# An LSTM on one core: other layouts and queues for the loads of Wx, Wh, x and h0 before the first step

## The chip, the core and the metric

The kernel runs on one core of a Trainium2 chip. A core has a matrix engine (PE, TensorE), a vector engine (DVE, VectorE), a scalar engine (ACT, ScalarE), GpSimd (POOL) and a queue engine that issues transfers (SP, SyncE). They run their own instruction streams and meet through semaphores. Transfers (DMAs) are issued by SP, ACT or POOL, and 16 DMA engines carry them between HBM and the on-chip memory SBUF, which has 128 partitions. Matmul results land in PSUM.

The metric is the device time in microseconds (us) of one execution. The profile's clock starts at the first instruction, and its "span" ends with the last one.

## The reference, cut to what matters

There are 16 sequences of 512 steps with 512 features; the hidden width is also 512. All data is float32.

```python
xW = einsum('ntd,dg->ntg', x, Wx) + b          # Wx: 512 x 2048
def step(carry, xw_t):
    prev_h, prev_c = carry
    a = xw_t + prev_h @ Wh                      # Wh: 512 x 2048
    i, f, o = sigmoid(a[:, :512]), sigmoid(a[:, 512:1024]), sigmoid(a[:, 1024:1536])
    g = tanh(a[:, 1536:])
    next_c = f * prev_c + i * g
    next_h = o * tanh(next_c)
    return (next_h, next_c), next_h
out = x + scan(step, (h0, 0), xW over t)        # h0 is cond_1024, 16 x 512
```

The 512 steps depend on each other through `h`. Before the first one, Wx (4 MB), Wh (4 MB), the first slice of x (256 KB), h0 (32 KB) and the bias must have come from HBM.

## The kernel before

**The loop.** `lstm_residual` (line 38 on) keeps the four gates of the 16 sequences in PSUM banks, with the width split into two halves, a and b, that work a little apart. Each of the 512 steps multiplies the previous h, as parts in float16, with `wq`, Wh split into three float16 parts (`products`, the matmuls of line 188), and in between projects x of a later pair of steps with Wx in float32 (`project`, line 165). DVE and ACT do the gates. `turn_x` (line 161) transposes the x of one pair of steps on DVE in 32 x 32 blocks, once in two steps. The order on every engine is that of the program; the framework adds the waits.

**The stretch before the loop.** Wh is loaded to `wh_sb` (line 134, in `load_w`) in eight copies of 512 KB, four from SP's queue and four from ACT's, each for a block of 32 partitions: the rows of two of the four 32-row chunks `c` that each block has. Chunks 0 and 1 come with the first four copies, chunks 2 and 3 with the second. Behind them, SP issues the eight copies of the first x slice (`load_xs(0)`, line 147), four of h0 (line 347), eight of Wx (line 134 again, 32 partitions each) and eight of the second x slice. POOL issues the bias as one row (`brow`, line 348) and as a tile (`bias`, line 352), and the other eight copies of Wx. ACT then loads its function table (line 371).

While a queue's instruction waits, everything behind it in that queue waits too. The framework gives each transfer one of a fixed set of completion semaphores in turn, and the next user of a semaphore waits until its last user has landed.

**The split of Wh.** `bound(c)` finds the largest magnitude in each row of chunk c (lines 397 to 399; ACT does chunk 1, DVE the others), `scales(h)` makes scale factors from the bounds of two chunks (lines 410 to 422), and `split(n, k)` with k = 0 to 4 makes the three float16 parts of half-chunk n (n = 0 to 7): k = 0, 2, 4 on ACT (lines 432, 439, 444), k = 1, 3 on DVE (lines 435, 442). A loop over n interleaves them. In it are also the three `turn_x` of the first x slice and the transpose of h0 to `hT0` (line 470), at n = 3 before the change; the first two projections (64 matmuls) and 16 matmuls of zeros (line 374) for PE, written at n = 4; and `seed(0, h)` (line 175, ACT), which puts the projection into the gates, at n = 6. The first step then starts on PE with `first_products` (line 201), which needs seeds and `hT0`.

Of the kernel before, what the change touches and what calls it, by code (L numbers as in the profile page):

```python
# [7 lines left out]
FP = mybir.dt.float32  # L8
HP = mybir.dt.float16
I32 = mybir.dt.int32  # L10
AF = mybir.ActivationFunctionType
ALU = mybir.AluOpType
PSUM = bass.MemoryType.PSUM

P = 128
Q = 32
# [15 lines left out]
def lstm_residual(ctx: ExitStack, tc: tile.TileContext, x, h0, wx, wh, b, out):  # L32
# [26 lines left out]
    nc = tc.nc  # L59
    N, T, D = x.shape  # L60
    H = h0.shape[1]
    NJ = H // P
    NK = D // P
    G = 4
    U = P // 2
    GU = G * U
    GH = G * H // 2
# [7 lines left out]
    const = ctx.enter_context(tc.tile_pool(name="const", bufs=1))  # L75
    tmp = ctx.enter_context(tc.tile_pool(name="tmp", bufs=3))
# [19 lines left out]
    wx_sb = const.tile([P, NK, G * H], FP, tag="wx", name="wx_sb")  # L96
    wh_sb = const.tile([P, NK, G * H], FP, tag="wh", name="wh_sb")
    wq = [const.tile([P, NK, G * H], HP, tag=f"wq{i}", name=f"wq{i}") for i in range(3)]

    wx_j = wx_sb.rearrange("p c (g j w) -> p c j g w", g=G, j=NJ)  # L100
    wh_j = wh_sb.rearrange("p c (e g j h u) -> p c e h j g u", e=2, g=2, j=NJ, h=2)
    wq_j = [w.rearrange("p c (g j h u) -> p c h j g u", g=G, j=NJ, h=2) for w in wq]
    bias = const.tile([P, G * P], FP, tag="bias", name="bias")
    mask = const.tile([P, S2], FP, tag="mask", name="mask")
    zero = const.tile([1, G * P], HP, tag="zero", name="zero")
    amax = const.tile([P, NK], FP, tag="amax", name="amax")
    top = const.tile([P, 2], FP, tag="top", name="top")
    bits = const.tile([P, 2, 2], FP, tag="bits", name="bits")
    sc = const.tile([P, 2, 4], FP, tag="sc", name="sc")
# [4 lines left out]
    parts = [  # L114
        [const.tile([P, 2, 5 * N], HP, tag=f"parts{h}{i}", name=f"parts{h}{i}") for i in range(2)]
        for h in range(2)
    ]
# [3 lines left out]
    ]  # L121
    xb = [psum.tile([P, G * P], FP, tag=f"xb{i}", name=f"xb{i}") for i in range(NXB)]

    def load_w(dst, w, c0, dmas, parts=1):


        n = G * H // parts
        for j in range(2):
            for q, dma in enumerate(dmas):
                r = w[(2 * q + j) * P + c0 * Q :][: 2 * Q].rearrange("(c u) f -> u c f", u=Q)  # L130
                p = slice((2 * q + j) * Q, (2 * q + j + 1) * Q)
                for e in range(parts):
                    a = parts - 1 - e
                    dma.dma_start(  # L134
                        out=dst[p, c0 : c0 + 2, a * n : (a + 1) * n],
                        in_=r[:, :, e * n : (e + 1) * n],
                    )

    xs = {}

    def load_xs(s, dma=nc.sync):

        xs[s] = xsp.tile([P, XP, P], FP, tag="xs", name=f"xs_{s}")
        for j in range(NJ):
            for r in range(S2):
                p0 = j * Q + r * N
                dma.dma_start(
                    out=xs[s][p0 : p0 + N],
                    in_=x[:, s * XB + r : (s + 1) * XB : S2, j * P : (j + 1) * P],
                )  # L150


    xT = {}
# [4 lines left out]
    def turn_x(q):  # L158
        s, i = divmod(q, XP)
        xT[q] = xtp.tile([P, NK, Q], FP, tag="xT", name=f"xT_{q}")  # L160
        nc.vector.transpose(xT[q].rearrange("p c m -> p (c m)"), xs[s][:, i])

    def project(q, c):
        for j in range(NJ):
            nc.tensor.matmul(  # L165
                xb[q % NXB][j * Q : (j + 1) * Q],
                lhsT=xT[q][:, c],
                rhs=wx_j[:, c, j],
                start=False,
                stop=(c == NK - 1),  # L170
                skip_group_check=True,
            )

    def seed(t, h):
        nc.scalar.mul(  # L175
            gates[h][t % 2][:, :GU].rearrange("p (g u) -> p g u", g=G),
            xb[t // 2 % NXB].rearrange("p (g h u) -> p h g u", g=G, h=2)[:, h],
            mask[:, t % 2 : t % 2 + 1],
        )
# [157 lines left out]
    warm = const.tile([1, 1], FP, tag="warm", name="warm")  # L337
    brow = const.tile([1, G * H], FP, tag="brow", name="brow")
    ones = const.tile([1, Q], FP, tag="ones", name="ones")
    for c in (0, 2):  # L340
        load_w(wh_sb, wh, c, (nc.sync, nc.scalar))
    load_xs(0)
    nc.vector.memset(zero, 0.0)
    nc.vector.memset(h_in, 0.0)
    nc.vector.memset(ones, 1.0)
    for j in range(NJ):
        nc.sync.dma_start(out=h_in[j * Q : j * Q + N], in_=h0[:, j * P : (j + 1) * P])
    nc.gpsimd.dma_start(out=brow, in_=b.rearrange("(o f) -> o f", o=1))
    b_j = b.rearrange("(o e g j w) -> j e o g w", o=1, e=2, g=2, j=NJ)
    for j in range(NJ):  # L350
        for e in range(2):
            nc.gpsimd.dma_start(
                out=bias[j * Q : (j + 1) * Q, (1 - e) * GU : (2 - e) * GU].rearrange(
                    "p (g w) -> p g w", g=2
                ),
                in_=b_j[j, e].broadcast_to([Q, 2, P]),
            )
    for c in (0, 2):
        load_w(wx_sb, wx, c, (nc.sync, nc.gpsimd), 2)
    load_xs(1)  # L360

    for h in range(2):
# [10 lines left out]
    def zeros(bank, start):  # L373
        nc.tensor.matmul(  # L374
            bank, lhsT=zero[:, :P], rhs=zero, start=start, stop=start, skip_group_check=True
        )
# [14 lines left out]
                    skip_group_check=True,  # L391
                )

    def bound(c):
        if c == 1:
            junk = tmp.tile([P, G * H], HP, tag="junk", name="junk", bufs=1)
            nc.scalar.activation(junk, wh_sb[:, c], AF.Abs, accum_out=amax[:, c : c + 1])
        else:
            nc.vector.tensor_reduce(
                amax[:, c : c + 1],  # L400
                wh_sb[:, c],
                mybir.AxisListType.X,
                ALU.max,
                apply_absolute_value=True,
            )

    def scales(h):


        nc.vector.tensor_tensor(  # L410
            top[:, h : h + 1], amax[:, 2 * h : 2 * h + 1], amax[:, 2 * h + 1 : 2 * h + 2], ALU.max
        )
        t = top[:, h : h + 1].bitcast(I32)
        e, inv = bits[:, h, 0:1], bits[:, h, 1:2]
        nc.vector.tensor_scalar(
            inv.bitcast(I32), t, EXP, EXP, ALU.bitwise_and, ALU.bitwise_xor
        )
        nc.vector.tensor_scalar(e.bitcast(I32), t, EXP, None, ALU.bitwise_and)
        nc.vector.tensor_scalar(RS2[h], inv, 2.0**12, 0.5, ALU.mult, ALU.min)
        nc.vector.tensor_scalar(RS[h], inv, 2.0**13, 1.0, ALU.mult, ALU.min)  # L420
        nc.vector.tensor_scalar(S[h], e, 2.0**-14, 1.0, ALU.mult, ALU.max)
        nc.vector.tensor_scalar(RSL[h], RS[h], 1.0 / LO, None, ALU.mult)
# [3 lines left out]
    def split(n, k):  # L426

        c, e = divmod(n, 2)
        w = wh_sb[:, c, e * GH : (e + 1) * GH]
        f = [q[:, c, (1 - e) * GH : (2 - e) * GH] for q in wq]  # L430
        if k == 0:
            nc.scalar.mul(f[0], w, RS2[c // 2])
        elif k == 1:
            r1[n] = tmp.tile([P, GH], FP, tag="r1", name=f"r1_{n}")
            nc.vector.scalar_tensor_tensor(
                r1[n], w, RS[c // 2], f[0], ALU.mult, ALU.subtract
            )
        elif k == 2:
            nc.scalar.copy(f[1], r1[n])
        elif k == 3:  # L440
            r2[n] = tmp.tile([P, GH], FP, tag="r2", name=f"r2_{n}")
            nc.vector.tensor_tensor(r2[n], r1[n], f[1], ALU.subtract)
        else:
            nc.scalar.mul(f[2], r2[n], LO)

    NH = 2 * NK
    bound(0)
    bound(1)
    scales(0)
    split(0, 0)  # L450
    split(0, 1)
    split(1, 0)
    for n in range(NH):
        if n == 0:
            bound(2)
        if n == 2:
            bound(3)
            scales(1)
        if n + 1 < NH:
            split(n + 1, 1)  # L460
        split(n, 2)
        split(n, 3)
        if n:
            split(n - 1, 4)
        if n + 2 < NH:
            split(n + 2, 0)
        if n == 3:
            for q in range(3):
                turn_x(q)
            nc.vector.transpose(hT0.rearrange("p c m -> p (c m)"), h_in)  # L470
        if n == 4:
            for c in range(NK):
                for q in range(2):
                    project(q, c)

            for _ in range(16):
                zeros(xb[3], False)
        if n == 6:
            for h in range(2):
                seed(0, h)  # L480
# [4 lines left out]
    for t in range(T):  # L485
        s, ti = divmod(t, XB)
        q, half = divmod(t + 4, 2)
# [12 lines left out]
        for op in STEP.split():  # L500
            name, h = op.split("_")
# [4 lines left out]
        if t % 2:  # L506
            for h in range(2):
                unscale(t // 2, h)
            if q + 1 < NP:
                turn_x(q + 1)  # L510
        else:
            if q + 1 < NP:
                put_bias(q + 1)
            if t:
                residual(t // 2 - 1)
# [33 lines left out]
```

## Time and profile before

| | |
|---|---|
| median of 3 runs | 2294.34 us (2294.26 to 2299.03) |
| the profiled execution | 2294.09 us |
| its span | 2291.7 us |
| PE busy | 2249.4 us (98%) |
| DVE busy | 1952.7 us (85%) |
| ACT busy | 1838.1 us (80%) |
| first matmul of step 0 (line 201) starts at | 50.80 us |

The profiled execution is 2.4 us longer than its span; this lies outside of what the engines show. Times in the text are counted from the span's start. A line of the profile such as "12.74 1.91 ACT L397 ... x1" says that ACT began an instruction of line 397 at 12.74 us and that it took 1.91 us. "[4.07 <-DMA wh_sb...]" says that the engine had been idle for 4.07 us before it and that the landing of that transfer ended the idle time. "SPq" and "ACTq" are the instruction queues that issue transfers.

### The profile page before, as it was taken

How to read it: one execution, taken by the hardware profiler on the slowest of the kernel's cores; microseconds unless marked ns; L12 is line 12 of the kernel's file. 1: busy time of each engine (PE TensorE's matmuls, PEld its weight loads, DVE VectorE, ACT ScalarE, POOL GpSimd, SP SyncE). 2: the span in 40 equal slices, each digit the busy share in tenths (PEclk: the TensorE clock that was granted, in tenths of full speed). 3: DMA queues.
4: the chain of work that ended last, by engine and by line, in shares of the span. 5: the costliest groups of instructions: out<-in, count | busy, mean ns of one | idle time of the engine just before them, and what ended most of it. 6: DMA issues, size and time to landing. Idle time of an engine off the chain costs nothing.

```text
span 2291.7 us, 137735 instructions
## 1 busy us (share of the span) xinstructions
PE 2249.4 (98%) x57445; PEld 1572.7 (69%) x57445; DVE 1952.7 (85%) x11813; ACT 1838.1 (80%) x7959; POOL 127.2 (6%) x281
## 2 busy tenths in 40 slices
PE   4999999999999999999999999999999999999997
PEld 2677766777766777777666777776677777666775
DVE  5888888888888888888888888888888888888887
ACT  5888888888888888888888888888888888888887
POOL 1000000000000000000000000000000000000000
PEclk9999999999999999999999999999999999999999
DMA  7000000100100001000001001010000010010000
GB/s 166 13 21 15 22 18 17 22 15 20 22 14 22 22 13 22 21 14 22 17 18 22 15 20 22 13 22 22 13 22 19 17 22 18 17 22 15 20 18 12
DMA packets 85005, 51.10 MB, mean 22 GB/s; under 512 B 17104, under 2 KB 82720, under 8 KB 83872
## 3 DMA queue, kind: packets, MB, share of 16 engines
q1 hardware_dynamic: 83008, 37.82, 7.6%
q8 instruction: 452, 7.41, 1.4%
q0 software_dynamic: 928, 2.37, 0.5%
q10 hardware_dynamic: 448, 2.13, 0.4%
q14 instruction: 169, 1.38, 0.2%
HBM read 25.47 MB, written 16.78 MB: 18 GB/s over the span
## 4 chain that ended last, share of the span: by engine, by line
PE 98%; DMA 2%; DVE 0%; issue 0%; ACTq 0%; POOLq 0%; POOL 0%; SPq 0%
PE gates L188 59%; PE xb L165 38%; DMA wh_sb<-in_L_cond_Wh_dram 1%; DMA xs<-in_x_dram 0%; DMA wx_sb<-in_L_cond_Wx_dram 0%; PE gates L201 0%; PE xb L374 0%; ACTq L134 0%; DVE gt L224 0%; DVE preo L231 0%; DVE pre L231 0%; DVE parts L284 0%; DVE gto L224 0%; POOLq L544 0%; POOL ob L326 0%
## 5 line engine op out<-in xcount | busy, mean ns | idle before, releaser
L188 PEld LDWEIGHTS <-parts 128*32 128x32 f16 x49056 | 1307.1, 96 | 368.8 <-DVE parts L284 298.8
L188 PE MATMUL gates<-wq,parts 128*32 128x256 f16 x49056 | 1449.2, 273 | 4.2 <-DVE parts L284 4.2
L165 PE MATMUL xb<-wx_sb,xT 128*32 128x512 f32 x8192 | 977.1, 593 | 22.5 <-DMA wx_sb<-in_L_cond_Wx_dram 22.5
L224 DVE STREAM_TRANSPOSE gt<-gates 128x192 f32<-128x192 f32 x1024 | 391.7, 383 | 229.9 <-PE gates L188 170.7
L165 PEld LDWEIGHTS xb<-wx_sb,xT 128*32 128x32 f32 x8192 | 264.6, 110 | 327.5 <-issue 303.5
L258 ACT ACTIVATE gc<-pre 128x32 f32<-128x32 f32 x1022 | 234.7, 230 | 274.7 <-DVE pre L231 261.9
L175 ACT ACTIVATE gates<-xb,mask 128x256 f32<-128x256 f32 x1024 | 450.3, 440 | 2.1 <-PE xb L165 2.1
L266 ACT ACTIVATE os<-so,sc 128x32 f32<-128x32 f32 x1024 | 329.1, 321 | 16.6
L288 ACT COPY parts<-parts 128x32 f16<-128x32 f16 x1022 | 214.4, 210 | 131.7 <-DVE parts L284 131.7
L231 DVE SCALAR_TENSOR_TENSOR pre<-gt 128x96 f32<-128x96 f32 x1024 | 253.6, 248 | 0.0
L260 ACT ACTIVATE sif<-pre 128x64 f32<-128x64 f32 x1024 | 245.7, 240 | 0.0
L326 POOL TENSOR_TENSOR ob<-hb,xs 128x128 f32<-128x128 f32 x256 | 117.1, 457 | 2146.0 <-DVE hb L325 1732.5
L224 DVE STREAM_TRANSPOSE gto<-gates 128x64 f32<-128x64 f32 x1024 | 229.6, 224 | 0.0
L276 ACT ACTIVATE tch<-gc 128x32 f32<-128x32 f32 x1024 | 226.8, 221 | 0.3
L298 DVE SCALAR_TENSOR_TENSOR parts<-rem,parts 128x32 f16<-128x32 f32 x1022 | 196.3, 192 | 35.5
L264 ACT ACTIVATE so<-preo 128x32 f32<-128x32 f32 x1024 | 226.4, 221 | 0.0
L231 DVE SCALAR_TENSOR_TENSOR preo<-gto 128x32 f32<-128x32 f32 x1024 | 192.6, 188 | 17.5
L290 DVE SCALAR_TENSOR_TENSOR parts<-parts,hist 128x32 f16<-128x32 f16 x1022 | 192.0, 188 | 17.7
L268 DVE TENSOR_TENSOR pr<-sif,gc 128x64 f32<-128x64 f32 x1022 | 204.2, 200 | 0.0
L284 DVE TENSOR_TENSOR parts<-os,tch 128x32 f16<-128x32 f32 x1022 | 196.5, 192 | 0.0
L274 DVE TENSOR_TENSOR gc<-pr 128x32 f32<-128x32 f32 x1024 | 192.1, 188 | 0.0
L278 DVE SCALAR_TENSOR_TENSOR hist<-os,tch 128x32 f32<-128x32 f32 x1024 | 188.7, 184 | 0.3 <-ACT tch L276 0.3
(47 smaller groups left out, 730.8 us busy)
## 6 DMA issues: line engine op xcount, KB each, us to landing
xs<-in_x_dram SPq DMA_DIRECT2D x512, 32.0 KB, 2.0
out_dram<-ob SPq DMA_DIRECT2D x504, 32.0 KB, 1.7
wh_sb<-in_L_cond_Wh_dram ACTq DMA_DIRECT2D x4, 512.0 KB, 13.4
wh_sb<-in_L_cond_Wh_dram SPq DMA_DIRECT2D x4, 512.0 KB, 13.1
wx_sb<-in_L_cond_Wx_dram POOLq DMA_DIRECT2D x8, 256.0 KB, 9.5
wx_sb<-in_L_cond_Wx_dram SPq DMA_DIRECT2D x8, 256.0 KB, 6.8
bias<-in_L_cond_b_dram POOLq DMA_DIRECT2D x8, 32.0 KB, 13.4
out_dram<-ob SPq DMA_DIRECT2D x8, 24.0 KB, 1.6
```

Source lines behind the costliest of these rows:

```text
L165: nc.tensor.matmul(xb[q % NXB][j * Q : (j + 1) * Q], lhsT=xT[q][:, c], rhs=wx_j[:, c, j], start=False, stop=(c == NK - 1), skip_group_chec ...
L175: nc.scalar.mul(gates[h][t % 2][:, :GU].rearrange("p (g u) -> p g u", g=G), xb[t // 2 % NXB].rearrange("p (g h u) -> p h g u", g=G, h=2)[: ...
L188: nc.tensor.matmul(g[j * Q : (j + 1) * Q, :GU], lhsT=a[:, cc, k * N : (k + 2) * N], rhs=wq_j[i - 1][:, 2 * kh + cc, h, j], start=False, st ...
L224: nc.vector.transpose(gt.rearrange("p b m -> p (b m)"), gates[h][t % 2][:, b0 * Q : b1 * Q])
L231: nc.vector.scalar_tensor_tensor(pre.rearrange("p g (c n) -> p (g c) n", c=2), gt[:, :, (1 - t % 2) * N : (2 - t % 2) * N], 1.0 / LO, gt[: ...
L258: nc.scalar.activation(gc[h][:, 0], v["pre", h][:, 0], AF.Tanh)
L260: nc.scalar.activation(new("sif", t, h, [P, 2, 2 * N]), v["pre", h][:, 1:3], AF.Sigmoid)
L264: nc.scalar.activation(new("so", t, h, [P, 2 * N]), v["preo", h][:, 0], AF.Sigmoid)
L266: nc.scalar.mul(new("os", t, h, [P, 2 * N]), v["so", h], S[h])
L268: nc.vector.tensor_tensor(new("pr", t, h, [P, 2, 2 * N]), v["sif", h], gc[h], ALU.mult)
L276: nc.scalar.activation(new("tch", t, h, [P, 2 * N]), gc[h][:, 1], AF.Tanh)
L288: nc.scalar.copy(slots(t, h, 2), slots(t, h, 0))
```

## The change

1. **x and h0 first.** SP's queue begins with the eight copies of the first x slice and the four of h0.
2. **Wh through POOL's queue.** Eight copies, one for each chunk c and each half e of the columns, in this order. Each fills all 128 partitions with 4 KB; on the HBM side its rows come in four blocks of 32.
3. **The bias through ACT's queue**: `brow` and the eight copies of `bias`.
4. **Wx with row 4p + c on partition p.** Eight copies on SP's queue, each over 128 partitions with 4 KB for each. Since the rows of Wx now stand on other partitions, `turn_x` reads x with a step of four elements, so that its transposes have the same order of rows.
5. **The bounds.** `bound(2)` moves from n = 0 to n = 1, and the bound of chunk 3 is shared: ACT does its first half, DVE the second, with one more column in `amax`. `scales` takes the maximum with a reduction over two or three columns.
6. **The transposes of x and h0** move from n = 3 to n = 1.

```diff
-    amax = const.tile([P, NK], FP, tag="amax", name="amax")
+    amax = const.tile([P, NK + 1], FP, tag="amax", name="amax")
...
-    def load_w(dst, w, c0, dmas, parts=1):
-        n = G * H // parts
-        for j in range(2):
-            for q, dma in enumerate(dmas):
-                r = w[(2 * q + j) * P + c0 * Q :][: 2 * Q].rearrange("(c u) f -> u c f", u=Q)
-                p = slice((2 * q + j) * Q, (2 * q + j + 1) * Q)
-                for e in range(parts):
-                    a = parts - 1 - e
-                    dma.dma_start(
-                        out=dst[p, c0 : c0 + 2, a * n : (a + 1) * n],
-                        in_=r[:, :, e * n : (e + 1) * n],
-                    )
+    wh_rows = wh.rearrange("(j c u) f -> c j u f", c=NK, u=Q)
+    wx_rows = wx.rearrange("(p c) f -> c p f", c=NK)
...
-        nc.vector.transpose(xT[q].rearrange("p c m -> p (c m)"), xs[s][:, i])
+        nc.vector.transpose(xT[q], xs[s][:, i].rearrange("p (u c) -> p c u", c=NK))
...
-    for c in (0, 2):
-        load_w(wh_sb, wh, c, (nc.sync, nc.scalar))
+    for c in range(NK):
+        for e in range(2):
+            f = slice(e * GH, (e + 1) * GH)
+            nc.gpsimd.dma_start(out=wh_sb[:, c, f], in_=wh_rows[c, :, :, f])
     load_xs(0)
...
-    nc.gpsimd.dma_start(out=brow, in_=b.rearrange("(o f) -> o f", o=1))
+    nc.scalar.dma_start(out=brow, in_=b.rearrange("(o f) -> o f", o=1))
...
-            nc.gpsimd.dma_start(
+            nc.scalar.dma_start(
                 out=bias[j * Q : (j + 1) * Q, (1 - e) * GU : (2 - e) * GU].rearrange(
...
-    for c in (0, 2):
-        load_w(wx_sb, wx, c, (nc.sync, nc.gpsimd), 2)
+    for c in range(NK):
+        for e in range(2):
+            nc.sync.dma_start(
+                out=wx_sb[:, c, (1 - e) * GH : (2 - e) * GH],
+                in_=wx_rows[c, :, e * GH : (e + 1) * GH],
+            )
     load_xs(1)
...
-    def bound(c):
-        if c == 1:
-            junk = tmp.tile([P, G * H], HP, tag="junk", name="junk", bufs=1)
-            nc.scalar.activation(junk, wh_sb[:, c], AF.Abs, accum_out=amax[:, c : c + 1])
+    def bound(i, c, on_act, f=slice(0, G * H)):
+        w = wh_sb[:, c, f]
+        if on_act:
+            junk = tmp.tile([P, G * H], HP, tag="junk", name=f"junk_{i}", bufs=1)
+            nc.scalar.activation(junk[:, f], w, AF.Abs, accum_out=amax[:, i : i + 1])
         else:
             nc.vector.tensor_reduce(
-                amax[:, c : c + 1],
-                wh_sb[:, c],
+                amax[:, i : i + 1],
+                w,
...
-        nc.vector.tensor_tensor(
-            top[:, h : h + 1], amax[:, 2 * h : 2 * h + 1], amax[:, 2 * h + 1 : 2 * h + 2], ALU.max
-        )
+        nc.vector.tensor_reduce(
+            top[:, h : h + 1], amax[:, 2 * h : 2 + 3 * h], mybir.AxisListType.X, ALU.max
+        )
...
-    bound(0)
-    bound(1)
+    bound(0, 0, False)
+    bound(1, 1, True)
...
-        if n == 0:
-            bound(2)
+        if n == 1:
+            bound(2, 2, False)
         if n == 2:
-            bound(3)
+            bound(3, 3, True, slice(0, GH))
+            bound(4, 3, False, slice(GH, 2 * GH))
             scales(1)
...
-        if n == 3:
+        if n == 1:
             for q in range(3):
                 turn_x(q)
             nc.vector.transpose(hT0.rearrange("p c m -> p (c m)"), h_in)
```

## The prediction

> **What bounds the kernel now.** I read the page's chain first, then the chain in order of time, then the timeline of the start, the waits and the DMA rates. By engine and line, the chain is:
>
> ```profile
> PE 98%; DMA 2%; DVE 0%; issue 0%; ACTq 0%; POOLq 0%; POOL 0%; SPq 0%
> ```
>
> PE's loop sets the end. All edits but one lie ahead of it; the 2% of DMA is what they can reach. The chain in order of time (start us, us, what):
>
> ```profile
> 2.16 19.91 DMA wh_sb<-in_L_cond_Wh_dram
> 22.44 9.42 DMA xs<-in_x_dram
> 31.88 6.03 DMA wx_sb<-in_L_cond_Wx_dram
> 38.05 9.27 PE xb L165 x64
> 47.31 3.56 PE xb L374 x16
> 50.87 3.63 PE gates L201 x128
> ```
>
> Three groups of loads in a row, then PE: projections, zeros, first products. From line 201's start at 50.80 us the loop runs on its own to 2291.7. So the question is: when does line 201 start after the change? The timeline shows the split that runs beside this:
>
> ```profile
> 12.74 1.91 ACT L397 ACTIVATE junk<-wh_sb 128x2048 f16<-128x2048 f32 x1 [8.30 <-DMA wh_sb<-in_L_cond_Wh_dram]
> 15.73 2.19 ACT L432 ACTIVATE wq<-wh_sb,sc 128x1024 f16<-128x1024 f32 x2 [0.99 <-DVE sc L419]
> 22.26 2.29 DVE L399 TENSOR_REDUCE amax<-wh_sb 128x1 f32<-128x2048 f32 x1 [4.07 <-DMA wh_sb<-in_L_cond_Wh_dram]
> 32.00 1.15 ACT L432 ACTIVATE wq<-wh_sb,sc 128x1024 f16<-128x1024 f32 x1 [1.11 <-DVE sc L419]
> 46.52 0.81 ACT L175 ACTIVATE gates<-xb,mask 128x256 f32<-128x256 f32 x2 [2.09 <-PE xb L165]
> ```
>
> The split begins at T0 = 15.73. At 22.26 DVE has lost 4.07 us to chunk 2. At 46.52 ACT's seeds have lost 2.09 to PE. The waits between queues (us in total, times, longest):
>
> ```profile
> SPq L147 <- DMA wh_sb<-in_L_cond_Wh_dram: 16.8, 4, 4.7
> POOL bias L352 <- DMA brow<-in_L_cond_b_dram: 4.7, 1, 4.7
> ```
>
> POOL's ninth transfer waited for its first, and SP's first x copy, the ninth of SP and ACT together, for the first Wh: each set has eight semaphores, and SP and ACT share one. DMA rates: first the queues between 20 and 24 us (packets, MB, share), then windows (PE, PEld, DVE, ACT, POOL, clock, DMA share, GB/s):
>
> ```profile
> q0 software_dynamic: 281, 0.76, 82.9%
> q1 hardware_dynamic: 266, 0.11, 14.4%
> 10.00:12.00 2.00, 1.80 (x20) 1.00 (x24) 0.00 (x0) 0.00 (x0) 0.53 (x1) 1.00 1.10 256
> 36.00:38.00 2.00, 0.00 (x0) 0.00 (x0) 2.00 (x6) 2.00 (x3) 0.00 (x0) 1.00 1.00 201
> ```
>
> The queues send equally many packets, POOL's of 4 KB and SP's of 512 B: the engines take one from each in turn. At full share they moved 256 GB/s of Wh and 201 of Wx.
>
> [...] Wx alone at 201 to 217; and the packet records show 8 KB in 0.309 us at the very start, about 0.54 later[...]. [...]
>
> **The change, part by part.** *Times of small copies.* SP issues an x copy in about 0.43 us, so the eight go out from 0.75 to 4.2. POOL's first issue was at 1.28 and took 0.66; with about 1 us to the first packet, Wh flows from 2.9. (Eight issues by 0.53 are 4.2 us; twice as many rows each, at worst 8.5: 512 KB in 1.06 us is 495 GB/s, still ahead of the engines.) By then three x copies are through. Before, beside 4 KB packets, the eight landed from 22.9 to 31.9, 1.13 us each, so five more end at 2.9 + 5 x 1.13 = 8.5, and about 9 with the landing. The four of h0 took 1.7 us: 10.7. `brow` takes x's fifth semaphore, `bias` those of x's last three, of h0 and of `brow`; so ACT's last issue is at about 11.3 to 11.5. Queued behind these waits are ACT's table load (1.28) and line 371 (0.20), then `bound(1)`: ACT is free at 13.0, against 12.74 when `bound(1)` ran before. This is the price of the bias on ACT, and it decides T0.
>
> *Rate of the large copies.* [...] 0.155 us for 4 KB by the short packets above, 425 GB/s[...]. I take 340 GB/s, 0.19 us, for all [...]; the other end is 0.31, the 32-partition value[...].
>
> *Wh.* Each engine carries 64 packets. Beside small copies a round is 0.19 + 0.05 us, so chunks 0 and 1 (32 packets) take 7.7: 10.6, landed 11.6. ACT at 13.0 is later, so T0 = 13.0 + (15.73 - 12.74) = 16.0, 0.3 later than before.
>
> *Wx* waits for `bias` semaphores and starts at about 10.5. From there rounds are 0.38: Wh's second 32 packets end at about 22.5 to 23.5. All 8.9 MB end at 2.9 + 8.9/0.34 = 29.1, landed 30.
>
> *The split.* From T0, DVE does k = 1 of n = 0 until 2.46; then 1.27 + 1.22 (n = 1, 0), bound(2) 2.28, 1.28 + 1.22 (n = 2, 1), the moved transposes 0.88, half a bound 1.2, scales to its scale 0.57: 12.4, less six overlaps of 0.1, plus 0.4 for the wider step of `turn_x`: 12.2. Chunk 2 is wanted at T0 + 4.8 = 20.8 and chunk 3 by ACT at T0 + 7.5 = 23.5: just there. So the first scaling by the second factor starts at 28.2, against 32.00 before. That gain of 3.8 is the 4.07 stall. Halving bound 3 saves 1.1, but the moved transposes use it up; ACT's half (1.0 + 0.19) hides in its wait for DVE. From 32.00 to the end of the first seeds there were 15.33, with 2.09 of waiting: 13.2. So seeds end at 28.2 + 13.2 = 41.4.
>
> *PE.* `hT0` is ready at T0 + 10.5 = 26.5. The projections take 9.27: 35.8; Wx's last chunk, used in their last quarter from 33.5, landed at 30. Zeros 3.6: 39.4. PE now waits 2 us for seeds; line 201 starts at 41.5 in place of 50.80: 9.3 earlier. What is late next is ACT: its last four jobs after the first seeds (about 4.1 us) end at 45.5, while line 258 of step 0 wants ACT 3.6 us after line 201's start, 45.1. That costs 0.4. Gain 8.9.
>
> *At no cost:* `turn_x` in the loop. Two lines of its timeline:
>
> ```profile
> 1100.18 0.30 DVE L161 STREAM_TRANSPOSE xT<-xs 128x128 f32<-128x128 f32 x1
> 1100.86 0.38 DVE L224 STREAM_TRANSPOSE gt<-gates 128x192 f32<-128x192 f32 x1 [0.38 <-PE gates L188]
> ```
>
> DVE then waits 0.38 for PE. Line 224's rows (383 ns for 192 columns, 224 for 64) give 1.24 ns for each, so 0.16 of the 0.30 is streaming; twice that is +0.16, hidden. With no cover it would be 253 x 0.16 = 40 us. The bounds of its cost: 0 to three times 0.16; I take 0.16. The second x slice comes after Wx on SP, near 32; wanted at step 3, 13 us after line 201. The new reduction in `scales` stands at the old 0.16.
>
> Sum for the profiled execution: 2294.09 - 8.9 = 2285.2. That execution lay 0.25 below the median of the runs, so the median after is forecast at **2285.4**.
>
> **Rivals.** *B: Wh on four engines[...]* (0.31 a packet, Wx 0.19). [...] against: [...] that four copies at once still cover 16 engines. Before Wx starts at 11.5, 24 packets at 0.36; eight more at 0.5: landed 16.5, T0 = 19.5; chunk 3 at 32.5, half bound and scales to 34.3, + 13.2: line 201 at 47.6, ACT 0.4: gain 2.8, **2291.5**.
>
> *C: both large streams at 0.31, and Wx in turn with Wh takes half its rate.* Before, Wh went ahead and was whole at 22; here chunk 3 comes at 37.4, seeds end at 52.4: **2296**, within the bound of no change. For: 201 to 256 GB/s is all that before shows.
>
> *D, the other sign: `turn_x` with its step.* Place: DVE in odd steps; it decides from 0.38 + 8.9/253 = 0.42 us extra. At four times the streaming, + 0.48: 0.10 a turn past the cover, 25 us: **2310**. Against: so high a factor has no row.
>
> *E: ACT held by its queue until 18* (small copies as slow as the 9 to 15 us of before). T0 = 21, line 201 at 46.5: **2290**. Against: those stood behind Wh in their own queue.
>
> **How the numbers follow.** Less than 0.2%, 4.6 us, can't be told from no change. Mine 0.66 (faster but for 0.01), own range 2282 to 2288: T0 from 13 to 18. B 0.20 (gain 0 to 6: a third faster), C 0.06 (same but for 0.01), D 0.05 (slower), E 0.03 (same). Faster 0.65 + 0.07 = 0.72; same 0.01 + 0.13 + 0.05 + 0.03 = 0.22; slower 0.06. The range reaches from my lower end to B's: 2282 to 2292; outside are C, D and my tails.
>
> **What would show it.** Right: POOL's eight Wh issues without waits; ACT's line 371 near 11.5 to 13; T0 near 16; over 300 GB/s from 10 to 25 us; no DVE wait for `wh_sb` after T0; PE waiting about 2 us for ACT before line 201 near 41.5; the loop still 4.36 us a step (line 224 from 1100.86 to 1105.22), 0.46 or less for line 161. Wrong: DMA below 250 GB/s and DVE waiting for chunk 3 (B, C); less idle before line 224 and a longer loop (D); ACT issuing bias past 15 (E).

## The result: slower, nearly all of it before the loop

The kernel after takes 2308.7 us (median of 6 runs, 2303.25 to 2314.65), against 2298.0 us for runs of the kernel before taken beside them. The ratio is 1.0052, 95% interval 1.0035 to 1.007: slower by 10.7 us between the medians, by about 12 us by the ratio, where 9 us faster was forecast. The profiled execution took 2308.88 us, its span is 2306.8 us, 15.1 us over that of before. The profile of before is of one of its fastest executions (2294.09 us; the medians of its runs beside the experiments below are 2297.7 to 2299.7), so the two profiles lie further apart than the runs do.

The chain of work that ended last, by engine, on the page of after:

```profile
PE 97%; DMA 2%; ACT 0%; DVE 0%; POOL 0%; issue 0%; POOLq 0%; DVEq 0%
```

and its first pieces in order of time (start us, us, what):

```profile
1.28 4.79 POOL wh_sb L332 x7
6.07 41.76 DMA wh_sb<-in_L_cond_Wh_dram
62.55 5.86 PE gates L190 x128
```

Before, the chain waited 19.9 us for Wh, then for x, then for Wx. Now it waits 41.8 us for Wh alone, and the first products (line 201 of before, line 190 here) start at 62.55 us in place of 50.80. The timeline of after shows where the split stood:

```profile
14.46 1.28 ACT L366 ACT_TABLE_LOAD   x1 [14.46 <-DMA bias<-in_L_cond_b_dram]
22.87 1.91 ACT L393 ACTIVATE junk<-wh_sb 128x2048 f16<-128x2048 f32 x1 [6.91 <-DMA wh_sb<-in_L_cond_Wh_dram]
25.47 2.19 ACT L428 ACTIVATE wq<-wh_sb,sc 128x1024 f16<-128x1024 f32 x2 [0.60 <-DVE sc L415]
36.29 2.29 DVE L395 TENSOR_REDUCE amax<-wh_sb 128x1 f32<-128x2048 f32 x1 [6.01 <-DMA wh_sb<-in_L_cond_Wh_dram]
47.85 1.22 DVE L395 TENSOR_REDUCE amax<-wh_sb 128x1 f32<-128x1024 f32 x1 [5.86 <-DMA wh_sb<-in_L_cond_Wh_dram]
49.75 1.15 ACT L428 ACTIVATE wq<-wh_sb,sc 128x1024 f16<-128x1024 f32 x1 [4.30 <-DVE sc L415]
62.08 0.78 ACT L164 ACTIVATE gates<-xb,mask 128x256 f32<-128x256 f32 x2
```

Each bound waits for its chunk; the last half of chunk 3 was taken up at 47.85 us, and the fifth scaling (49.75) has to wait for its bound.

| us from the span's start | before | after |
|---|---|---|
| the split begins (T0) | 15.73 | 25.47 |
| fifth scaling | 32.00 | 49.75 |
| first products start | 50.80 | 62.55 |
| first products take | 3.70 | 5.86 |
| DVE reads the first gates | 53.70 | 67.62 |
| from there to the end of the span | 2238.0 | 2239.2 |

So 13.9 of the 15.1 us had been lost when DVE read the first gates: 11.75 by the late start and about 2.2 because the first products ran slower. The loop and the end added 1.2.

The windows of after (PE, PEld, DVE, ACT, POOL, clock, DMA share, GB/s) show why Wh is late:

```profile
12.00:14.00 2.00, 0.00 (x0) 0.00 (x0) 0.00 (x0) 0.00 (x0) 0.00 (x0) 1.00 1.04 142
42.00:44.00 2.00, 2.00 (x16) 0.56 (x12) 0.00 (x0) 1.60 (x3) 0.00 (x0) 1.00 1.03 395
64.00:66.00 2.00, 2.00 (x48) 1.84 (x44) 1.08 (x1) 1.67 (x2) 0.00 (x0) 0.50 0.00 0
```

With only Wh and small copies under way, all 16 engines are busy (share 1.04) and yet carry 142 GB/s, 129 of it Wh. With Wx alone, in equally large copies of 4 KB rows, they carry 395. In the packet records a 4 KB packet of Wh takes a median of 0.43 us between 10 and 16 us; one of Wx takes 0.16 us after 40 us. Wh's own packets were not slow at first: between 3 and 7 us, while POOL is still issuing the eight copies, their median is 0.159 us. The third window shows the first products at half the clock (0.50).

### The profile page after: what moved, and what is told of

It reads as the page before. It is cut to its first block, busy times and chain, and to the rows that moved or that the text cites. A ratio compares the mean times of both kernels' runs of the same rounds, so it can differ in the third digit from the quotient of the medians.

```text
span 2306.8 us, 137723 instructions
## 1 busy us (share of the span) xinstructions
PE 2253.6 (98%) x57445; PEld 1572.6 (68%) x57445; DVE 1979.5 (86%) x11813; ACT 1839.1 (80%) x7961; POOL 123.5 (5%) x272
## 3 DMA queue, kind: packets, MB, share of 16 engines
q0 software_dynamic: 4224, 4.21, 1.2%
HBM read 25.47 MB, written 16.78 MB: 18 GB/s over the span
## 4 chain that ended last, share of the span: by engine, by line
PE 97%; DMA 2%; ACT 0%; DVE 0%; POOL 0%; issue 0%; POOLq 0%; DVEq 0%
PE gates L177 59%; PE xb L154 38%; DMA wh_sb<-in_L_cond_Wh_dram 2%; PE gates L190 0%; POOL wh_sb L332 0%; ACT wq L440 0%; ACT wq L428 0%; ACT wq L435 0%; DVE amax L395 0%; DVE r L431 0%; DVE gt L213 0%; DVE r L438 0%; DVE preo L220 0%; DVE pre L220 0%; DVE parts L273 0%
## 5 line engine op out<-in xcount | busy, mean ns | idle before, releaser
L154 PE MATMUL xb<-wx_sb,xT 128*32 128x512 f32 x8192 | 977.2, 593 | 32.5 <-DVE xT L150 32.5
## 6 DMA issues: line engine op xcount, KB each, us to landing
h_in<-in_cond_dram SPq DMA_DIRECT2D x4, 8.0 KB, 10.7
```

The costliest lines, as they stand in the source:

```text
L154: nc.tensor.matmul(xb[q % NXB][j * Q : (j + 1) * Q], lhsT=xT[q][:, c], rhs=wx_j[:, c, j], start=False, stop=(c == NK - 1), skip_group_chec ...
```

## The experiments

Two theories about Wh. **F**: because a copy has four blocks on the HBM side, it runs on four engines only, and many such copies at once bring no more than a few. **Rivals**: POOL's path is slow for large copies (P); or reading four blocks 1 MB apart is slow (H). Four kernels tell these apart.

### e1_rows: 128 rows on the HBM side of Wh

```diff
-    wh_rows = wh.rearrange("(j c u) f -> c j u f", c=NK, u=Q)
+    wh_rows = wh.rearrange("(p c) f -> c p f", c=NK)
...
-            nc.gpsimd.dma_start(out=wh_sb[:, c, f], in_=wh_rows[c, :, :, f])
+            nc.gpsimd.dma_start(out=wh_sb[:, c, f], in_=wh_rows[c, :, f])
```

> The kernel after, but Wh too is read with row 4p + c on partition p (the h parts are not reordered, so the recurrence uses Wh's rows in another order than the reference). Bytes, queue and copy sizes are those of after; the HBM side has 128 rows as its slowest dimension in place of four blocks. Theory F (a copy with four blocks runs on four DMA engines[...]): chunks 0 and 1 landed by 11 to 13 us, over 300 GB/s, chunk 3 by 25, line 190 starts at 41 to 45 us in place of 62.55, time 16 to 20 us below after (about 0.99 to 0.995 of before). Rival P (POOL's path is slow for large copies): as after, 140 to 160 GB/s, line 190 at 60 to 63. Rival H (four blocks 1 MB apart in HBM are slow to read): fast, as F.

Measured: 2287.46 us, ratio 0.9953 (0.9938 to 0.9968). In its windows (same columns), with Wh and small copies:

```profile
8.00:12.00 4.00, 0.77 (x8) 0.00 (x0) 2.29 (x1) 1.69 (x3) 0.00 (x0) 1.00 1.05 346
```

and in its timeline, T0, the fifth scaling and the first products:

```profile
14.40 2.19 ACT L428 ACTIVATE wq<-wh_sb,sc 128x1024 f16<-128x1024 f32 x2 [0.60 <-DVE sc L415]
26.59 1.15 ACT L428 ACTIVATE wq<-wh_sb,sc 128x1024 f16<-128x1024 f32 x1 [1.73 <-DVE sc L415]
39.40 6.32 PE L190 MATMUL gates<-wh_sb,hT 128*32 128x128 f32 x128 [2.89 <-ACT gates L164]
```

As many bytes through the same queue in eight copies of the same size go at 346 GB/s (312 of it Wh) instead of 142, and the first products start 23 us earlier than in after. P falls. F and H both stand, since the rows that a copy reads lie differently in HBM too.

### e3_pitch: four blocks at another distance

```diff
-            nc.gpsimd.dma_start(out=wh_sb[:, c, f], in_=wh_rows[c, :, :, f])
+            r = wh[16 * c : 16 * c + 4 * 144] if False else wh[16 * c :][: 3 * 144 + Q]
+            src = bass.AP(tensor=r.tensor, offset=r.offset + e * GH, ap=[[144 * G * H, NJ], [G * H, Q], [1, GH]])
+            nc.gpsimd.dma_start(out=wh_sb[:, c, f], in_=src)
```

> The kernel after, with four blocks of 32 rows in each copy of Wh as before, but the blocks 144 rows (1.125 MB) apart in HBM in place of 128 (1 MB); so some rows of Wh are used twice and some not at all. Theory F: nothing gained, 140 to 165 GB/s from 10 to 28 us, line 190 at 58 to 65 us. Rival H: over 210 GB/s, line 190 before 52.

(The first branch of `r` is never taken.)

Measured: 2318.25 us in one run; 151 GB/s from 12 to 16 us, 115 to 132 from 16 to 28 us; first products at 67.94 us. It is somewhat slower still than expected under F (58 to 65), and nothing was gained: the distance of just 1 MB in HBM isn't the cause. Other distances were not tried; e4_hw, next, bears on H again.

### e4_hw: the four-block copies on the queues of before

```diff
-    for c in (0, 2):
-        load_w(wh_sb, wh, c, (nc.sync, nc.scalar))
+    wh_rows = wh.rearrange("(j c u) f -> c j u f", c=NK, u=Q)
+    for c in range(NK):
+        for e, dma in enumerate((nc.sync, nc.scalar)):
+            f = slice(e * GH, (e + 1) * GH)
+            dma.dma_start(out=wh_sb[:, c, f], in_=wh_rows[c, :, :, f])
```

> The kernel before, but its eight copies of Wh have the shape that after gives them (one chunk, half the columns, four blocks, 128 partitions), still on SP's and ACT's queues. Theory F[...]: DMA share about 0.25 while Wh loads, 55 to 110 GB/s, Wh landed at 40 to 80 us, line 201 at 60 to 100 us. If the four blocks are spread over all engines: share 1.0 and Wh landed by 18 to 23 us, as before. Rival H: share 1.0 at 140 to 160 GB/s, Wh landed near 30.

Measured: 2330.52 us in one run, first products at 83.0 us. Its window with Wh and what is left of Wx on POOL's queue:

```profile
28.00:32.00 4.00, 0.00 (x0) 0.00 (x0) 0.00 (x0) 0.00 (x0) 0.00 (x0) 1.00 0.25 103
```

A share of 0.25 is four engines of sixteen, for all queues together: SP's and ACT's copies use the same four. Of the 103 GB/s, 74 are Wh. Each packet takes 0.159 us, as the first ones of after did, so reading four blocks 1 MB apart isn't slow in itself.

### e5_two: two four-block copies in flight

```diff
+    seen = const.tile([1, 2], FP, tag="seen", name="seen")
     for c in range(NK):
         for e in range(2):
             ...
+        nc.gpsimd.tensor_tensor(seen, wh_sb[0:1, c, GH - 1 : GH + 1], wh_sb[0:1, c, GH - 1 : GH + 1], ALU.add)
```

> The kernel after, but POOL issues Wh two copies at a time: after each pair a tiny addition on POOL reads an element of both and so waits until they have landed. With copies on four engines, a pair uses eight of the sixteen. Theory F ([...] more of them bring nothing): while only Wh is loading 120 to 190 GB/s at a DMA share near 0.5, 4 KB packets at 0.16 to 0.25 us, and chunk 3 landed at 35 to 48 us, no later than in after (47.85). Rival N (the packets of Wh are slow by themselves, 0.3 to 0.5 us, whoever else is at work): half the rate of after, 70 to 80 GB/s, chunk 3 at 60 us or later.

Measured: 2327.25 us in one run. Its windows with the first pair:

```profile
8.00:12.00 4.00, 0.77 (x8) 0.00 (x0) 0.00 (x0) 0.00 (x0) 0.00 (x0) 1.00 0.54 145
12.00:16.00 4.00, 0.00 (x0) 0.00 (x0) 1.25 (x1) 1.49 (x2) 0.95 (x3) 1.00 0.25 66
```

At half the share, two copies move as much (145 GB/s, 121 of it Wh) as all eight in after (142), with packets of 0.22 us in place of 0.43. So the packets aren't slow by themselves, as rival N had it; past two copies, more engines at work bring nothing but longer packets. The packet records have 7 to 8 packets of the first pair under way at once: POOL's copies do go to different sets of four, which SP's and ACT's don't. The landing I had expected wrong: chunk 3 came at 66 us, not 35 to 48. The first pair thins out in the second window (26 of the 66 GB/s are Wh), none of Wh is under way from 14 to 18 us, and then Wx took turns with the second pair.

POOL's four-block copies also have some 400 packets of 4 bytes each, where those of e1_rows have 16 (4224 packets on POOL's queue in after, 1152 there). Their own time is small, 0.05 of the engines' from 10 to 16 us.

What stretches the packets from 0.16 to 0.43 us when eight such copies are in flight is not shown by any run here.

### e11_wxlast: how much Wx's turns cost

```diff
-            nc.sync.dma_start(
+            nc.gpsimd.dma_start(
                 out=wx_sb[:, c, (1 - e) * GH : (2 - e) * GH],
```

> The kernel after, but Wx is issued on POOL's queue behind Wh (and on POOL's semaphores), so that it can't take turns with Wh. If Wx's turns cost Wh its second half: chunks 0 and 1 by 21 to 24 us as in after, chunk 3 by 31 to 37 us in place of 47.85, fifth scaling at 36 to 40 in place of 49.75; Wx lands by 45 to 49 and PE's zeros then end at 49 to 54, so line 190 starts at 49 to 54 us, 8 to 13 us earlier than in after. If the four-engine copies are that slow whoever else is at work: chunk 3 again at 43 us or later, line 190 at 58 or later.

Measured: 2303.44 us in one run, span 2299.8 us, 7.0 us below that of after.

```profile
39.25 1.15 ACT L428 ACTIVATE wq<-wh_sb,sc 128x1024 f16<-128x1024 f32 x1 [1.68 <-DVE sc L415]
53.68 5.37 PE L190 MATMUL gates<-wh_sb,hT 128*32 128x128 f32 x128
```

Chunk 3's halves were taken up at 34.53 and 37.40 us and the fifth scaling came at 39.25, 10.5 us earlier than in after; 1.7 of this was there at T0 already (23.77 in place of 25.47). The first products start at 53.68, 8.9 us earlier, and are now held by PE's zeros (50.13 to 53.75) behind the late Wx. So of the 11.75 us that the start was late in after, about 9 come back when Wx can't take turns with Wh.

This is no second cause beside the slow copies. In e1_rows Wx stands where it stands in after, but its packets begin at 16 us, when Wh is nearly through, and the first products start at 39.40. In after the two meet from 28 to 38 us because Wh is late; from 30 to 36 us Wx sends 183 packets and Wh 109.

### e2_blocks: a valid layout with sixteen engines

```diff
     for c in range(NK):
-        for e in range(2):
-            f = slice(e * GH, (e + 1) * GH)
-            nc.gpsimd.dma_start(out=wh_sb[:, c, f], in_=wh_rows[c, :, :, f])
+        for j in range(NJ):
+            nc.gpsimd.dma_start(out=wh_sb[j * Q : (j + 1) * Q, c], in_=wh_rows[c, j])
```

> The kernel after, but Wh in 16 copies of 256 KB, one for each chunk and block: 32 partitions, neighbouring HBM rows, 8 KB each, still on POOL's queue. Theory F: all 16 engines[...]: chunk 1 by 13 to 16 us, chunk 3 by 26 to 31, line 190 at 44 to 49 us; 2 to 7 us faster than before. Rival P: 140 to 160 GB/s, as after. Rival H: fast, as F.

Measured: 2290.91 us, ratio 0.997 (0.9959 to 0.9981).

```profile
8.00:12.00 4.00, 0.77 (x8) 0.00 (x0) 1.29 (x1) 1.00 (x1) 1.42 (x3) 1.00 1.05 218
43.75 5.70 PE L190 MATMUL gates<-wh_sb,hT 128*32 128x128 f32 x128 [0.94 <-ACT gates L164]
```

From 4 to 16 us 205 to 219 GB/s are moved, ACT has chunk 1 at 16.15 us, and the first products start at 43.75 us: at the edges of what F gave. A copy of 32 partitions is slower than e1_rows (346), and still the change as a whole is now faster than before.

### e8_zeros and e9_warm: the slower first products

In e2_blocks the first products took 5.70 us, at a granted clock of 0.50 from 44 to 46 us, although PE had stood idle for only 0.94 us. Two edits of it:

```diff
-            for _ in range(16):
+            for _ in range(22):
                 zeros(xb[3], False)
```

> As e2_blocks, with 22 matmuls of zeros before the first products in place of 16, so that PE has no idle time before them. Theory W (PE slows down when it stands idle, and that makes the first products 5.7 to 6.3 us in place of 3.7): line 190 in 3.6 to 4.2 us. Rival: these zeros do not keep PE fast; line 190 again 5.5 us or more and begins up to 1.5 us later.

```diff
-            for _ in range(16):
-                zeros(xb[3], False)
+            for i in range(20):
+                nc.tensor.matmul(
+                    xb[3][i % NJ * Q : (i % NJ + 1) * Q],
+                    lhsT=xT[0][:, i // NJ % NK],
+                    rhs=wx_j[:, i // NJ % NK, i % NJ],
+                    start=False,
+                    stop=False,
+                    skip_group_check=True,
+                )
```

> As e2_blocks, with the 16 matmuls of zeros (one row of weights) replaced by 20 float32 matmuls of the projection's own kind (128 rows) into the same spare bank, which the bias copy overwrites later. Theory W2 (it is matmuls of zeros on a single row that let PE fall to half speed): line 190 takes 3.6 to 4.2 us in place of 5.70, the first gates come about 1.5 to 2 us earlier, 0.9955 to 0.997 of before. Rival: PE's speed there has another cause; line 190 again above 5 us, time as e2_blocks.

The windows of e8_zeros (the granted clock of PE stands before the DMA share):

```profile
38.00:40.00 2.00, 2.00 (x13) 0.85 (x10) 1.75 (x2) 2.00 (x3) 0.00 (x0) 1.00 0.17 43
42.00:44.00 2.00, 2.00 (x6) 0.46 (x4) 1.61 (x2) 2.00 (x5) 0.00 (x0) 0.50 0.02 6
```

and of e9_warm:

```profile
42.00:44.00 2.00, 0.94 (x28) 0.66 (x28) 1.53 (x2) 2.00 (x5) 0.00 (x0) 1.00 0.00 0
44.00:46.00 2.00, 2.00 (x82) 2.00 (x78) 1.23 (x1) 1.67 (x3) 0.00 (x0) 1.00 0.00 0
```

With more zeros PE is busy without a pause from 36.23 us on, and its clock falls to half all the same: the first products take 5.79 us (2292.73 us in one run). With projection matmuls on 128 rows, PE even idles for 1.06 us, the clock stays at 1.00 and the first products take 3.70 us. So in e2_blocks it is these matmuls of zeros that don't hold the clock. They differ from the others in three ways, a single row, float16 and data of zeros; which of them counts was not tried. e9_warm measured 2289.8 us, ratio 0.9957 (0.9944 to 0.9971), 1.1 us below the median of e2_blocks, with overlapping intervals; of the 2 us gained at the first products 0.6 is given back, since DVE reads the second step's gates 5.1 us after the first's there, and 4.5 in e2_blocks. It has the lowest median of the kernels that keep the reference's order of rows, and beats both before and after.

In the profile of before, with the same zeros, PE was still at full clock at this place (1.00 from 48 to 54 us), and in e10_order below, with before's loads and its projections 0.1 us later, it was not (0.71 from 48 to 52 us, 0.50 from 52 to 56). Why is not shown.

### e7_wx and e10_order: the other parts alone

In e7_wx, before has Wx's eight copies over 128 partitions on SP's queue behind h0, and the stepped transposes:

```diff
-    for c in (0, 2):
-        load_w(wx_sb, wx, c, (nc.sync, nc.gpsimd), 2)
+    wx_rows = wx.rearrange("(p c) f -> c p f", c=NK)
+    for c in range(NK):
+        for e in range(2):
+            nc.sync.dma_start(
+                out=wx_sb[:, c, (1 - e) * GH : (2 - e) * GH],
+                in_=wx_rows[c, :, e * GH : (e + 1) * GH],
+            )
...
-        nc.vector.transpose(xT[q].rearrange("p c m -> p (c m)"), xs[s][:, i])
+        nc.vector.transpose(xT[q], xs[s][:, i].rearrange("p (u c) -> p c u", c=NK))
```

> The kernel before with the Wx part alone: eight copies over 128 partitions with row 4p + c on partition p, all on SP's queue behind h0, and the step of four in the transposes of x. Wh, bias and the order of the split are as before. Theory: the loop's period stays 4.36 us (transposes at 0.41 us are hidden), Wx moves at 340 to 400 GB/s once Wh has landed, x is no longer held up by POOL's Wx packets, line 201 starts 1 to 6 us earlier than 50.8: 0.997 to 0.9995 of before. Rival D (the stepped transposes cost in the loop): slower than before by 3 us or more.

Measured: 2300.35 us, ratio 1.0001 (0.9992 to 1.001). Its windows with Wx (PE, PEld, DVE, ACT, POOL, clock, DMA share, GB/s), and its transposes of x (ns, least, median, most):

```profile
32.00:36.00 4.00, 0.00 (x0) 0.00 (x0) 4.00 (x5) 3.62 (x4) 0.00 (x0) 1.00 1.03 419
```

```profile
L161 DVE STREAM_TRANSPOSE xT<-xs x256: 370/411/425, 36.6 to 2266.3; 128x128 f32<-128x128 f32 x128
```

While Wx loads, 419 GB/s are moved, twice as many as before (201 to 217). But its copies stand behind x and h0 on SP and start late, so the projections start only 1.0 us earlier (37.07), and then PE loses its clock among the zeros (a mean of 0.58 from 48 to 52 us): these took 4.87 us (3.62 before) and the first products 5.75, starting at 51.19. Beside the profile of before, the expected gain is eaten there. The transposes are 0.11 us longer (0.304 before) and hidden: a step still takes 4.36 us in the median. From DVE's first gates to the end of the span it is 2241.3 us, against 2238.0 in before and 2240.5 in e10_order, which keeps the short transposes. Rival D, which needed some 25 us there, falls.

e10_order has before's loads and, of the change, parts 5 and 6 alone:

```diff
-    bound(0)
-    bound(1)
+    bound(0, 0, False)
+    bound(1, 1, True)
...
-        if n == 0:
-            bound(2)
+        if n == 1:
+            bound(2, 2, False)
         if n == 2:
-            bound(3)
+            bound(3, 3, True, slice(0, GH))
+            bound(4, 3, False, slice(GH, 2 * GH))
...
-        if n == 3:
+        if n == 1:
             for q in range(3):
                 turn_x(q)
```

> The kernel before with part 5 and part 6 alone: bound(2) at n = 1, the bound of chunk 3 shared by ACT and DVE, the transposes of x and h0 at n = 1. Loads as before. Expected: DVE no longer stalls for chunk 2 at n = 0, but now stalls at n = 1 for x and h0, which land at 32 and 33.5 us; the fifth scaling starts at 33 to 36 us (32.00 before); line 201 stays at 50 to 52 us, since Wx at 38 sets it; ratio 0.999 to 1.002.

Measured: 2299.84 us, ratio 0.9999 (0.9991 to 1.0007).

```profile
47.46 4.88 PE L374 MATMUL xb<-zero 1*128 1x512 f16 x16
52.27 5.73 PE L201 MATMUL gates<-wh_sb,hT 128*32 128x128 f32 x128
```

DVE waited 4.0 and 1.9 us for x and h0 at n = 1; the fifth scaling stood at 35.83 us; Wx (the projections begin at 38.15, as they did before) and the slower zeros set the start, at 52.27, just past the 50 to 52 that I gave. Otherwise as expected: with x and h0 behind Wh, moving the transposes forward brings nothing.

### e6_rings: an attempt to mend e2_blocks that made it worse

```diff
+    nc.scalar.dma_start(out=brow, in_=b.rearrange("(o f) -> o f", o=1))
     for c in range(NK):
         for j in range(NJ):
-            nc.gpsimd.dma_start(out=wh_sb[j * Q : (j + 1) * Q, c], in_=wh_rows[c, j])
+            dma = nc.gpsimd if j < 2 else nc.scalar
+            dma.dma_start(out=wh_sb[j * Q : (j + 1) * Q, c], in_=wh_rows[c, j])
...
-    nc.scalar.dma_start(out=brow, in_=b.rearrange("(o f) -> o f", o=1))
...
-            nc.scalar.dma_start(
+            nc.gpsimd.dma_start(
                 out=bias[j * Q : (j + 1) * Q, (1 - e) * GU : (2 - e) * GU].rearrange(
```

> As e2_blocks (16 copies of 32 partitions), but the blocks of the upper 64 partitions go through ACT's queue right behind the bias row and those of the lower 64 through POOL's[...]; the bias tile moves back to POOL behind Wh. Theory F: at least the 240 to 256 GB/s of before, chunk 1 by 12 to 14.5 us (16.15 in e2_blocks), chunk 3 by 21 to 24, line 190 at 40 to 43 us, 1 to 3 us faster than e2_blocks. Against it: ACT issues more and gets to its table later; then T0 stays at 17 to 19 and nothing is gained.

Measured: 2316.32 us, ratio 1.0073 (1.0058 to 1.0088). The waits of ACT:

```profile
ACT L366 <- DMA xs<-in_x_dram: 35.1, 1, 35.1
```

None of the numbers that I gave was right: T0 was 39.12. ACT's eight Wh copies took semaphores from the set that SP uses for x, h0 and Wx; ACT issued the last at 34.8 us and only then came to its table (35.14) and to `bound(1)` (36.54). This is rival E of the prediction, at a price that I hadn't thought of.

## Why the prediction was wrong, point by point

**The step that failed** is the rate of the large copies: "I take 340 GB/s, 0.19 us, for all". This was my estimate: below the 425 GB/s worked out from the first short packets, and above the 256 and 201 that before had shown at full share. I had four engines a copy in rival B and gave it 0.20, because four copies at once still cover all engines. e4_hw shows the four engines (a share of 0.25); e5_two and after show that covering all engines doesn't help: two copies in flight move 145 GB/s, eight 142. Measured: 0.43 us a packet and 142 GB/s in place of 0.19 and 340. With 128 rows on the HBM side the number holds: 346 GB/s in e1_rows.

**Rival B had the right number of engines and the wrong size.** Copies of this shape do run on four engines each (shares of 0.25 in e4_hw, 0.54 for two copies in e5_two); why many at once are slow stays open. B took 0.31 us, the value of 32 partitions in before, as the worst. With 0.43 us, chunk 1 was taken up at 22.87 (16.5 in B), and chunk 3 at 47.85 (32.5), so line 190 came at 62.55 (47.6). Both B and C were cheaper than what happened: I had bounded the unknown price from above by the worst row of before, which had another access pattern, and this gave the range its upper end.

**That Wx would take turns with Wh** was in B and C, and in my own sum as rounds of 0.38 us. It carries about 9 of the 11.75 us by e11_wxlast, but because the slow packets kept Wh under way until 38 us: in e1_rows, at about the rate that I took, Wx begins when Wh is nearly through.

**The small copies.** ACT came to its table at 14.46 in after and at 9.69 in e1_rows; 11.5 was forecast. The order in which the eight shared semaphores are given out was not mine (`brow` went first, at 0.74), h0 landed late, and Wx was issued from 22.74 us on in place of 10.5, but none of these set the end.

**The split and the seeds** held to the tenth in e1_rows: 26.59 - 14.40 = 12.19 us from T0 to the fifth scaling (12.2 forecast), and from there to the end of the first seeds, at 39.71, 13.12 us (13.2).

**The gain with sixteen engines** was 0.9953 of before, about 10.8 us, against the 8.9 forecast: T0 came 1.6 us earlier than forecast, and PE's clock (0.50 from 40 to 44 us) cost some. That the totals lie this close is in part luck.

**The clock** I missed: PE's first products at half clock (0.50 from 64 to 66 us) are 2.2 us of the difference between the two profiles. e10_order has them too (5.73 us) with before's loads, so they aren't shown to be a cost of the change.

**`turn_x`** cost nothing that shows in the loop, as forecast: 0.41 us (0.46 or less forecast), a step of 4.36 us.

## What to carry to other kernels

Before a copy is reshaped, look at the blocks on its HBM side: four of them put each of these copies on four engines (a share of 0.25 in e4_hw), though it filled 128 partitions, and 142 GB/s were moved in place of the 346 of e1_rows, with 128 rows there. A price for a pattern that no row shows isn't bounded by the worst row of another pattern; measure it alone first, or leave the range open on that side. And a load off the path, here Wx, can still take half the turns or more from the load on the path, once the two meet (183 packets against 109 from 30 to 36 us): its place in the queues is part of the price.

## What the runs showed that I had not expected

- More than two four-engine copies at once did not add up: 145 GB/s with two in flight on POOL's queue, 142 with eight; on SP's and ACT's queues all used the same four engines, with 103 GB/s in all.
- A busy PE can lose its clock: 22 float16 matmuls of zeros on one row left it at 0.50, while 20 float32 matmuls on 128 rows with a pause of 1.06 us behind them left it at 1.00.
- A transpose of 128 x 128 whose source steps by four elements took 0.41 us in place of 0.30.
- SP and ACT share eight semaphores for their transfers here: putting Wh on ACT behind x on SP held up ACT's first work until 35 us (one wait of 35.1 us for x).
